# Gated cross-attention block: loads, first pass, heads' weights and last batch reordered, and normalised inputs turned in blocks through memory

## The chip, the cores and the metric

The kernel runs on one core of one Trainium2 chip. The metric is the device time of one execution in microseconds, the median of three runs. One core has five instruction streams that are spoken of here: TensorE (PE, matrix products; PEld is its weight load), VectorE (DVE), ScalarE (ACT), GpSimd (POOL) and SyncE (SP), which here only issues DMA transfers.

## The reference

The inputs are `x` of 32 batches x 256 tokens x 256 channels and `ctx_1024` of 32 x 77 x 256, all float32. Cut to what matters (LN is a layer norm without gain, `proj(t) = (LN(t) * ln_g + ln_b) @ w_in.T` split into 8 heads of 128):

```python
f_q, f_k = proj(LN(x)), proj(ctx)          # values are the keys' features
cosine = f_q . f_k / (|f_q| |f_k|)
ratio  = 2*min(var,1)/(var+1)              # per token and head, of queries and of keys
var_component = outer(q_ratio, k_ratio)
decorr = exp(-5 * norm(offdiag(cov of f_q over ALL tokens)) / 128**2)    # per head
cw, vw, ww = softmax(mlp(mean of f_q, mean of f_k over ALL tokens))      # per head
mixed  = cw*cosine + vw*cosine*decorr + ww*var_component
x = x + tanh(g_xattn) * ((mixed @ f_k) @ w_out.T + b_out)

q, k, v = LN(x)@Wq, LN(x)@Wk, LN(x)@Wv     # 16 heads of 16
z = softmax(k.q / 16) @ v @ Wo             # softmax over queries, per key
z = gelu(l2norm(l2norm(z) @ Wff))
x = x + tanh(g_ffn) * z
```

The weights of the three components depend on sums over all tokens of all batches. So a first pass over the whole of `x` and `ctx` has to be finished before any batch can be.

## The kernel before

**Order of work.** All compute instructions are issued through a helper (class `InOrder`, line 30, which is why the profile gives line 30 for nearly all) that keeps the order of the program on each engine. Only DMA issues on SP may be placed by the scheduler. So the order in which stages are called is the order in which each engine meets them. A stage is a function of a batch `b`; `run(b, stage, ...)` calls it once.

**Buffers.** PSUM has three tiles called `mm` (512 columns each) that all products take in turn: the fourth use waits until the first is read out. Two more tile pairs, `sc`, hold attention scores, one, `zp`, the mixed values.

**First pass** (lines 678 to 961). `x` is loaded two batches at a time (`load_group`, eight buffers). For each of 64 row blocks of 128 tokens (two to a batch) DVE takes statistics (`x_stats`), POOL turns them into scales for four blocks (`x_scales`), ACT normalises (`x_norm`), PE adds the block to the 256 x 256 Gram matrix `gram` (`x_gram`). Other first-pass work is put between by a table, `between`: transposes of `w_in` and `w_out`, statistics, norm and transposes of the context in five pieces (`ctx_stats`, `ctx_norm`, `ctx_transpose` into `kT_all`), loads of the last layers' weights, centring of `w_in` (`centre_w_in`). Small parameters are loaded at the start by SP, after `w_out` and two pieces of context.

**Heads' weights** (lines 966 to 1136). From the Gram matrix come the covariance (`correlate`, `square_up`), the softmax of the three weights and the factor `aw`. Stages of batches 0 and 1 are called between these, and then a list of stages brings batch 0 up to its second attention.

**Main loop** (lines 1176 to 1243). The list `cycle` is run through once for each batch in its second attention; entries name how far ahead another batch is. A turn has, in order, scores and exponents of the present batch in four quarters (`scores`, `exponents`, `scale_values`, `mix_values`), the last layers of the previous one (`ff_out`, `ff_norm_first`, `ff_norm_second`, `ff_gelu`, `ff_add`), the first attention of the next (`query_ratios`, `query_scores`, `attend`, `ff_stats`, `ff_norm`, `ff_transpose`, `ff_project`, `ff_values`) and features of the one after (`transpose_inputs`, `query_features`, `scale_queries`, `turn_queries`, `weigh_keys`, `scale_keys`, `transpose_keys`, `key_outputs`); `key_features`, `norm_inputs`, `measure_keys` and `align_keys` are for three ahead.

**The stages the change touches.** `norm_inputs` (195): POOL normalises the batch into `xn`. `transpose_inputs` (206): four PE transposes of 128 x 128 into an `mm` tile, two DVE passes that apply gain and bias into `xTc`. `query_features` (372): products of `xTc` with `winT` into `fq`, read out by ACT (first half) and DVE (second). `key_features` (225): the same for keys into `fvx`, by ACT. `measure_keys` (243): statistics of keys, eight `bn_stats` and small DVE work, and one power on POOL into `nrx`; it has work only when a block of 128 key rows is full. `align_keys` (253): DMAs that bring a batch's 77 keys to partition 0 (`fv`, `nr`). `turn_queries` (404): for batches from 2 on, DVE transposes blocks of 32 x 32 (`fb`), one DMA writes them to memory (`fd`), four read them back into place (`fqT`). `ff_norm_first` (601): a power on POOL gives `i1`, two ACT squares of `u` use it. `query_scores` (353): its read-outs into `s` are by ACT, DVE, ACT. `ff_gelu` and `warm_exponentials` (617, 623): the GELU and a dry exponential, each of which brings a table load on ACT.

Of the kernel before, what the change touches and what calls it, by code (L numbers as in the profile page):

```python
# [33 lines left out]
def gated_block_kernel(  # L34
# [171 lines left out]
    def transpose_inputs(b):  # L206
        k = kept[b]
        pt = transpose_in(k["xn"])
        xT = pa.tile([P, 2, S], F32, tag="xTc", name="xTc", bufs=1)
        for c in range(2):  # L210
            dve.tensor_scalar(
                xT[:, c, :], pt[:, c * S : (c + 1) * S], gcol[:, c : c + 1],
                bcol[:, c : c + 1], ALU.mult, ALU.add,
            )
        k["xTc"] = xT
# [347 lines left out]
    def mix_values(b, u):  # L563
        k = kept[b]
        g, kt = u // 2, u % 2
        if u == 0:
            k["zp"] = ps_z.tile([P, 2, S], F32, tag="zp", name="zp")
        es = [k.pop(("e", u, jp)) for jp in range(2)]
        for i in range(2):
            for j in range(4):  # L570
                pe.matmul(
                    k["zp"][32 * j : 32 * j + 32, g, :],
                    lhsT=vzs[u % 2][:, j, 2 * i : 2 * i + 2, :].rearrange("p i d -> p (i d)"),
                    rhs=es[j // 2][:, j % 2, i, :],
                    start=(i == 0 and kt == 0),
                    stop=(i == 1 and kt == NT - 1),
                )
        if u == 3:
            zT = pa.tile([P, 2, S], F32, tag="zT", name="zT", bufs=1)
            dve.tensor_copy(zT, k.pop("zp"))  # L580
            k["zT"] = zT
# [51 lines left out]


# [44 lines left out]
    load_group(1)  # L679
    load_group(2)  # L680
    load_w_in(0)
    load_group(3)
    load_w_in(1)
    load_ctx(0)
    load_w_out()
    load_ctx(1)

    grow = sw.tile([P, D], F32, name="grow")
    nc.sync.dma_start(out=grow, in_=ln_g.partition_broadcast(P))
    w1_n = sw.tile([P, D], F32, name="w1_n")  # L690
    nc.sync.dma_start(out=w1_n, in_=wp_w1)
    w2_n = sw.tile([3, P], F32, name="w2_n")
    nc.sync.dma_start(out=w2_n, in_=wp_w2)
    b1_r = sw.tile([1, P], F32, name="b1_r")
    nc.sync.dma_start(out=b1_r, in_=wp_b1.unsqueeze(0))
    b2_r = sw.tile([1, 3], F32, name="b2_r")
    nc.sync.dma_start(out=b2_r, in_=wp_b2.unsqueeze(0))
    bo_n = sw.tile([1, D], F32, name="bo_n")
    nc.sync.dma_start(out=bo_n, in_=b_out.unsqueeze(0))
    wpg = sw.tile([H, P], F32, name="wpg")  # L700
    nc.sync.dma_start(out=wpg, in_=wp_ln_g.partition_broadcast(H))
    wpb = sw.tile([H, P], F32, name="wpb")
    nc.sync.dma_start(out=wpb, in_=wp_ln_b.partition_broadcast(H))
# [11 lines left out]
    def x_stats(g):  # L715
        for k in range(4 * g, 4 * g + 4):
# [4 lines left out]
    def x_scales(g):  # L721


        cols = slice(4 * g, 4 * g + 4)
# [31 lines left out]
    def ctx_stats(g):  # L756
# [12 lines left out]
        mvs[g] = mv, r  # L769

    def ctx_norm(g):
        ct = cts[g]
        mv, r = mvs[g]
        for t, rows in ctx_parts(g):
            (dve if t < 2 else pool).tensor_scalar(
                ct[0:rows, t, :], ct[0:rows, t, :], mv[0:rows, t, 0:1], r[0:rows, t : t + 1],
                ALU.subtract, ALU.mult,
            )
# [74 lines left out]
    def centre_w_in(c):  # L853
        if c == 0:
            wcs.append(sw.tile([P, 2, HD], F32, tag="wB", name="wc"))
# [5 lines left out]
            wcs[0][:, c, :].rearrange("p (h d) -> p h d", d=P),  # L861
# [28 lines left out]
    def set_constants():  # L890
# [21 lines left out]
        for vz in vzs:  # L912
# [5 lines left out]
        1: [(transpose_w_in, 0, 0), (transpose_w_in, 1, 0), (load_ff, (w_of[:, :, 0:D], Wo))],  # L918
        2: [(ctx_stats, 0), (transpose_w_in, 0, 1), (transpose_w_in, 1, 1)],
        3: [(ctx_norm, 0), (transpose_w_out, 0), (transpose_w_out, 1)],  # L920
        4: [(ctx_stats, 1), (transpose_w_out, 2), (transpose_w_out, 3)],
        5: [(ctx_norm, 1), (ctx_transpose, 0, 0), (ctx_transpose, 0, 1), (load_ctx, 2)],
        6: [(centre_w_in, 0), (load_ff, (wf_n, Wff))],
        7: [(ctx_transpose, 1, 0), (ctx_transpose, 1, 1), (load_ctx, 3), (ctx_stats, 2)],
        8: [(ctx_norm, 2), (transpose_wo,)],
        9: [(ctx_stats, 3), (transpose_predictor,)],
        10: [(ctx_norm, 3), (ctx_transpose, 2, 0), (ctx_transpose, 2, 1), (load_ctx, 4)],
        11: [(centre_w_in, 1), (multiply_wo_wff,)],
        12: [
            (ctx_transpose, 3, 0), (ctx_transpose, 3, 1), (ctx_stats, 4),  # L930
            (load_ff, *((ffw[n], w) for n, w in zip("qkv", (Wq, Wk, Wv)))),
        ],
        13: [(ctx_norm, 4), (gate,)],
        14: [(ctx_transpose, 4, 0), (ctx_transpose, 4, 1), (lay_out_bias,)],
    }

    for g in range(-2, NG):
        if g + 2 < NG:
            x_stats(g + 2)
            x_scales(g + 2)  # L940
        if g == -1:
            for k in range(3):
                x_norm(k)
        if g < 0:
            continue
        extra = between.get(g, [])
        for i in range(4):
# [4 lines left out]
            if i < len(extra):  # L952
                stage, *which = extra[i]
                stage(*which)
        if g + 4 < NG:
            load_group(g + 4)
        elif g + 4 < NG + 2:
            for b in (2 * (g + 4 - NG), 2 * (g + 4 - NG) + 1):
                run(b, load_queries)
        if g == NG - 2:  # L960
            run(0, norm_inputs)

    wc = wcs[0]
# [13 lines left out]
    dve.tensor_copy(bl[:, :, 1], lb[:, :, 0])  # L977
    pt = mm_tile()
# [3 lines left out]
    lbT = sw.tile([P, 2 * D], F32, tag="fc", name="lbT", bufs=2)[0:2]  # L982
# [8 lines left out]
    run(0, transpose_inputs)  # L991
    run(1, norm_inputs)
    pt = mm_tile()
# [14 lines left out]
    run(0, query_features, 0, 0)  # L1008
    pt = mm_tile()
# [17 lines left out]
    y = sw.tile([P, 2, HD], F32, tag="wA", name="y")  # L1027

    def correlate(co, hh):
        cs = slice(hh * 512, (hh + 1) * 512)  # L1030
        pt = mm_tile()
        for c in range(2):
            pe.matmul(
                pt, lhsT=gs[:, c, co * P : (co + 1) * P], rhs=wc[:, c, cs],
                start=(c == 0), stop=(c == 1),
            )
        if co == 0:
            dve.tensor_copy(y[:, co, cs], pt)
        else:
            act.copy(y[:, co, cs], pt)  # L1040
# [30 lines left out]
    def square_up(hh):  # L1071
        pt = mm_tile()
        for i in range(4):
            hs = slice((hh * 4 + i) * P, (hh * 4 + i + 1) * P)
            for c in range(2):
                pe.matmul(
                    pt[:, i * P : (i + 1) * P], lhsT=wc[:, c, hs], rhs=y[:, c, hs],
                    start=(c == 0), stop=(c == 1),
                )
        fc = sw.tile([P, 4, P], F32, tag="fc", name="fc", bufs=2)  # L1080
# [29 lines left out]
    run(0, query_features, 1, 1)  # L1110
    pt = mm_tile()
# [6 lines left out]
    run(0, key_features)  # L1118
    run(0, measure_keys)
    run(0, align_keys)  # L1120

# [3 lines left out]
    pool.tensor_tensor(hw, hw, phalf, ALU.pow)  # L1125
    dg = sw.tile([H, 2, H], F32, name="dg")
# [3 lines left out]
    run(0, turn_queries, 0)  # L1130
# [9 lines left out]
    run(0, scale_queries, 1)  # L1140
    run(1, query_features, 0, 0)
    run(0, transpose_keys, 0)
    run(0, transpose_keys, 1)
    run(1, query_features, 0, 1)
    for pair in (2, 0, 1):
        run(0, key_outputs, pair)
    run(1, key_features)
    run(0, turn_queries, 1)
    run(0, query_ratios)
    for pair in range(3):  # L1150
# [5 lines left out]
    run(0, ff_norm, 0)  # L1156
    run(1, query_features, 1, 0)
    run(0, attend, 1)
    run(0, ff_stats, 1)
    run(0, ff_norm, 1)  # L1160
    run(1, query_features, 1, 1)
    run(1, weigh_keys)
    run(1, scale_keys)
    run(1, scale_queries, 0)
    run(1, scale_queries, 1)
    run(0, ff_transpose)
    run(0, ff_project, "k")
    run(0, ff_project, "q")
    run(0, ff_values)

# [9 lines left out]
        (2, transpose_inputs),  # L1180
# [3 lines left out]
        (0, exponents, 0, 1),  # L1184
        (2, query_features, 0, 0),
# [13 lines left out]
        (2, scale_queries, 0),  # L1199
        (2, query_features, 1, 0),  # L1200
# [5 lines left out]
        (2, turn_queries, 0),  # L1206
# [5 lines left out]
        (-1, ff_gelu),  # L1212
        (2, warm_exponentials),
# [8 lines left out]
        (1, ff_transpose),  # L1222
        (0, scores, 3),
# [4 lines left out]
        (3, norm_inputs),  # L1228
        (2, turn_queries, 1),
        (3, measure_keys),  # L1230
        (3, align_keys),
# [5 lines left out]
        (0, scale_values, 3),  # L1237
        (-1, ff_add),
    ]
    for n in range(-4, B + 1):  # L1240
        for ahead, stage, *which in cycle:
# [36 lines left out]
```

## Time and profile before

| | |
|---|---|
| median of 3 runs | 1453.61 us (1453.37 to 1454.99) |
| the profiled execution, its own time | 1451.74 us |
| its span | 1450.0 us |
| busy PE, DVE, ACT, POOL | 1387.5, 1056.7, 906.3, 534.5 us |
| mean granted PE clock | 0.98 |
| bytes moved by DMA | 106.23 MB, 73 GB/s |
| first product of the Gram matrix, last | 9.1 us, 83.0 us |
| length of a turn of the main loop | 40.0 us (40.8 with a second half of keys) |
| first scores of the last batch, its last exponent, end | 1406.0, 1431.3, 1450.0 us |

The profile is of one execution on the chip. A row of the timeline reads: start, length, engine, line, operation, what it writes <- what it reads, and in brackets the idle time before it and what ended that. A row of the waits reads: who waited <- for whom, us in total, times, longest. A piece of the chain reads: start, length, engine and what it wrote. "xN" counts instructions; each float32 product is two of them. A matmul's length includes its way through the pipeline, so the starts, not the lengths, tell how PE's time is used.

### The profile page before, as it was taken

The page shows a single profiled execution, that of the slowest core. Times are in us where ns is not written, and L with a number is a line of the kernel's source. Part 1 is how long each engine was busy: PE and PEld are TensorE (multiplying, and loading weights), DVE is VectorE, ACT ScalarE, POOL GpSimd, SP SyncE. Part 2 cuts the span into 40 slices and gives each one's busy share as a digit, 9 for nine tenths or more (in the row PEclk, how much of TensorE's full clock was granted, in tenths as well). Part 3 has the DMA queues.
Part 4 walks back from the last instruction along what each step waited for, and adds up shares of the span by engine and source line. Part 5 has one row for each costly group of instructions (what it writes and reads, how often), then busy time and mean ns, then how long its engine had stood idle before and what let it go on. Part 6 is the DMA issues. An engine that isn't in the chain of part 4 may idle for free.

```text
span 1450.0 us, 25957 instructions
## 1 busy us (share of the span) xinstructions
PE 1387.5 (96%) x8833; PEld 812.5 (56%) x8833; DVE 1056.7 (73%) x3053; ACT 906.3 (63%) x2978; POOL 534.5 (37%) x660
## 2 busy tenths in 40 slices
PE   6898899999999999999999999999999999999985
PEld 5764555555555555555555555555555555555541
DVE  5734678787778787887777777778777777877743
ACT  4712356676666676667667667666666765766675
POOL 5922343343233333343333343433433333334210
PEclk9989999999999999999999999999999999999996
DMA  8500022211222222212222222222222211222100
GB/s 267 181 15 28 4 74 75 78 65 62 78 74 63 80 86 76 82 67 76 67 76 74 73 69 79 85 76 74 68 75 73 78 61 64 76 72 70 66 8 15
DMA packets 69395, 106.23 MB, mean 73 GB/s; under 512 B 10810, under 2 KB 46575, under 8 KB 69262
## 3 DMA queue, kind: packets, MB, share of 16 engines
q1 hardware_dynamic: 68430, 104.56, 22.2%
q8 instruction: 70, 1.15, 0.3%
q14 instruction: 63, 0.52, 0.1%
q10 hardware_dynamic: 832, 0.00, 0.0%
HBM read 54.44 MB, written 39.85 MB: 65 GB/s over the span
## 4 chain that ended last, share of the span: by engine, by line
PE 72%; ACT 14%; DVE 5%; issue 2%; DMA 1%; POOL 1%; SPq 0%; ACTq 0%; POOLq 0%
PE mm L30 56%; PE sc L30 10%; ACT e L30 7%; PE zp L30 7%; ACT L30 4%; DVE nm L30 3%; ACT u L30 1%; ACT fvx L30 1%; DMA fd<-fb 1%; POOL rs L30 0%; ACT dry L30 0%; DVE fb L30 0%; DVE qst L30 0%; DMA fqT<-fd 0%; ACT ge L30 0%
## 5 line engine op out<-in xcount | busy, mean ns | idle before, releaser
L30 ACT ACTIVATE e<-sc,nm 128x256 f32<-128x256 f32 x1024 | 472.7, 485 | 200.3 <-DVE nm L30 200.3
L30 DVE TENSOR_REDUCE nm<-sc 128x4 f32<-128x1024 f32 x256 | 301.4, 1219 | 50.6 <-PE sc L30 50.6
L30 PE MATMUL mm<-winT,xTc 128*128 128x512 f32 x512 | 237.5, 606 | 2.6 <-DVE xTc L30 2.6
L30 ACT ACTIVATION_READ_ACCUMULATOR e<-sc,nm 128x1 f32 x1024 | 221.6, 216 | 0.0
L30 POOL TENSOR_TENSOR rq<-qt,nhalf 128x8 f32<-128x8 f32 x64 | 105.3, 1645 | 272.2 <-DVE qt L30 272.2
L30 PEld LDWEIGHTS mm<-winT,xTc 128*128 128x128 f32 x512 | 95.1, 191 | 120.9 <-issue 93.2
L30 PE MATMUL sc<-q,kTf 32*128 32x512 f32 x1024 | 154.3, 648 | 5.8 <-ACT e L30 5.8
L30 PE MATMUL mm<-vw,s 128*128 128x256 f32 x640 | 146.8, 384 | 0.0
L30 PE MATMUL zp<-e,vz 128*32 128x256 f32 x2048 | 139.7, 391 | 5.1 <-DVE vz L30 4.4
L30 POOL TENSOR_SCALAR i<-nn 128x2 f32<-128x2 f32 x64 | 14.1, 221 | 344.4 <-ACT ge L30 344.4
L30 PEld LDWEIGHTS mm<-vw,s 128*128 128x128 f32 x640 | 119.0, 190 | 28.5 <-issue 13.7
L30 POOL TENSOR_TENSOR fq<-fq,rq 128x1024 f32<-128x1024 f32 x64 | 121.4, 1897 | 5.0
L30 PE MATMUL mm<-w_of,zT 128*128 128x512 f32 x256 | 117.9, 604 | 0.8 <-DVE zT L30 0.8
L30 PEld LDWEIGHTS zp<-e,vz 128*32 128x32 f32 x2048 | 59.0, 111 | 95.5 <-issue 37.3
L30 DVE BATCH_NORM_STATS2 qst<-fq 128x6 f32<-128x128 f32 x512 | 104.7, 278 | 0.0
L30 PE MATMUL mm<-woutT,fvT 128*64 128x256 f32 (+2 forms) x1024 | 99.2, 383 | 0.6 <-DVE fvT L30 0.5
L30 PE MATMUL mm<-fqT,fvT 128*64 128x256 f32 (+2 forms) x1024 | 93.9, 383 | 1.0 <-DMA fqT<-fd 1.0
L30 POOL TENSOR_SCALAR rs<-mv 128x1 f32<-128x1 f32 x64 | 33.1, 517 | 166.8 <-DVE mv L30 132.7
L30 DVE RECIPROCAL sums<-sums 128x8 f32<-128x8 f32 x128 | 24.6, 192 | 92.4 <-ACT e L30 92.3
L30 ACT COPY vw<-mm 128x512 f32<-128x512 f32 x32 | 18.8, 586 | 115.7 <-PE mm L30 115.7
L30 ACT ACT_TABLE_LOAD x64 | 82.1, 1283 | 7.7 <-DMA x<-in_x_dram 4.3
L30 POOL TENSOR_SCALAR xn<-x,mv_x,rstd_x 128x256 f32<-128x256 f32 x64 | 78.9, 1239 | 10.3 <-issue 10.3
(204 smaller groups left out, 2286.2 us busy)
## 6 DMA issues: line engine op xcount, KB each, us to landing
fd<-fb SPq DMA_DIRECT2D x60, 512.0 KB
fqT<-fd SPq DMA_DIRECT2D x240, 128.0 KB
x<-in_x_dram SPq DMA_DIRECT2D x64, 256.0 KB
out_dram<-x SPq DMA_DIRECT2D x32, 256.0 KB
fv<-fvx SPq DMA_DIRECT2D x13, 308.0 KB
ct<-in_ctx_dram SPq DMA_DIRECT2D x4, 512.0 KB
w_in_n<-in_L_xattn_w_in_dram SPq DMA_DIRECT2D x2, 512.0 KB
w_out_n<-in_L_xattn_w_out_dram SPq DMA_DIRECT2D x1, 1024.0 KB
```

The costliest lines, as they stand in the source:

```text
L30: return lambda *args, **kw: self._tc.keep_in_program_order(method(*args, **kw))
```

## The change

- **First pass.** Loads: halves of `w_in` come earlier; `w_out`, the second context piece and the small parameters are called from the table `between` and no longer at the start; each group of `x` is called for after the second row block of a turn instead of after the fourth. Statistics and scales of the first four row blocks are made two by two. `ctx_norm` gives its four blocks to POOL, ACT, DVE, ACT (before: two to DVE, two to POOL), for which POOL works out a negative mean. The table has the context earlier: the last piece's norm stands in turn 12 and its transposes in turn 14 (before 13 and 14).
- **Heads' weights.** `wc`, `y`, `lbT` and `fc` move to other buffers, so that `fvx` is free sooner; key features, statistics and alignment of batch 0, its query turn and its keys' transposes are called earlier, as are stages of batches 1 and 2.
- **Inputs.** For batches from 3 on, `transpose_inputs` is a DVE block transpose of `xn` into `xb`, one DMA to memory (`xd`) and four DMAs back into `xq`. A new stage `gain_inputs` applies gain and bias on POOL, at the end of the turn. `norm_inputs` and `transpose_inputs` are called for three ahead.
- **Main loop.** `measure_keys` and `align_keys` are called near the start of a turn for two ahead (before: near its end for three ahead). `ff_gelu` and `warm_exponentials` stand behind `ff_transpose`. `turn_queries` stands behind `key_outputs` and behind the last `scale_values`.
- **Last batch.** It has a list of its own, `last`: scores ahead of mixing, the GELU of batch 30 after its last exponents. `zT` is copied in two halves, and a new stage `ff_finish` ends the batch one row block at a time.

```diff
     def transpose_inputs(b):
-        k = kept[b]
-        pt = transpose_in(k["xn"])
+        k = kept[b]
+        if b < 3:
+            k["xq"] = transpose_in(k["xn"]).rearrange("p (c s) -> p c s", c=2)
+            gain_inputs(b)
+            return
+        k["xq"] = pa.tile([P, 4, NT, 2, 32], F32, tag="xq", name="xq", bufs=1)
+        xb = pa.tile([P, 4, NT * 2, 32], F32, tag="xb", name="xb", bufs=1)
+        dve.transpose(
+            xb.rearrange("p j n a -> p n j a"),
+            k["xn"].rearrange("p t (c j a) -> p (t c) j a", c=2, a=32),
+        )
+        xd = dram.tile([P, 4, NT * 2 * 32], F32, tag="xd", name="xd")
+        nc.sync.dma_start(out=xd, in_=xb.rearrange("p j n a -> p j (n a)"))
+        for j in range(4):
+            nc.sync.dma_start(
+                out=k["xq"][32 * j : 32 * j + 32].rearrange("p i t c a -> p i (t c a)"),
+                in_=xd[:, j].rearrange("(i p) n -> p i n", p=32),
+            )
+
+    def gain_inputs(b):
...
         for c in range(2):
-            dve.tensor_scalar(
-                xT[:, c, :], pt[:, c * S : (c + 1) * S], gcol[:, c : c + 1],
-                bcol[:, c : c + 1], ALU.mult, ALU.add,
-            )
+            if b < 3:
+                engine, out, src = dve, xT[:, c, :], xq[:, c, :]
+            else:
+                engine = pool
+                out = xT[:, c, :].rearrange("p (t i a) -> p i t a", t=NT, a=32)
+                src = xq[:, :, :, c, :]
+            engine.tensor_scalar(
+                out, src, gcol[:, c : c + 1], bcol[:, c : c + 1], ALU.mult, ALU.add
+            )
...
     load_group(1)
+    load_w_in(0)
     load_group(2)
-    load_w_in(0)
+    load_w_in(1)
     load_group(3)
-    load_w_in(1)
     load_ctx(0)
-    load_w_out()
-    load_ctx(1)
...
-            (dve if t < 2 else pool).tensor_scalar(
...
+            if t % 2:
+                act.activation(c, c, AF.Identity, bias=nm[0:rows, t : t + 1], scale=r_t)
+            else:
+                (dve if t == 2 else pool).tensor_scalar(
...
     cycle = [
...
         (0, scores, 0),
-        (2, transpose_inputs),
+        (3, norm_inputs),
...
         (0, exponents, 0, 1),
+        (2, measure_keys),
+        (2, align_keys),
         (2, query_features, 0, 0),
...
         (2, scale_queries, 0),
+        (3, transpose_inputs),
         (2, query_features, 1, 0),
...
-        (2, turn_queries, 0),
         (1, attend, 0),
...
-        (-1, ff_gelu),
-        (2, warm_exponentials),
         (1, ff_norm, 0),
...
         (1, ff_transpose),
+        (-1, ff_gelu),
+        (2, warm_exponentials),
         (0, scores, 3),
...
         (2, key_outputs, 1),
-        (3, norm_inputs),
-        (2, turn_queries, 1),
-        (3, measure_keys),
-        (3, align_keys),
+        (2, turn_queries, 0),
         (0, exponents, 3, 0),
...
         (0, scale_values, 3),
+        (2, turn_queries, 1),
+        (3, gain_inputs),
         (-1, ff_add),
     ]
+
+    last = [
...
+        (0, exponents, 3, 1),
+        (0, scale_values, 3),
+        (0, mix_values, 3),
+        (-1, ff_gelu),
+        (0, ff_out, 0),
+        (0, ff_out, 1),
+        (-1, ff_add),
+        (0, ff_finish),
+    ]
-    for n in range(-4, B + 1):
-        for ahead, stage, *which in cycle:
+    for n in range(-4, B):
+        for ahead, stage, *which in last if n == B - 1 else cycle:
```

## The prediction

> **What bounds the kernel now.** I read the page first (shares, slices), then the list of waits, then one full turn of the main loop in the timeline, engine by engine, then the chain of work at both ends.
>
> ```profile
> PE 1387.5 (96%) x8833; PEld 812.5 (56%) x8833; DVE 1056.7 (73%) x3053; ACT 906.3 (63%) x2978; POOL 534.5 (37%) x660
> PE   6898899999999999999999999999999999999985
> PEclk9989999999999999999999999999999999999996
> ```
>
> The slices show three stages: of slices 1 to 5 (36 us each) only one is full, the next 33 are full of TensorE (PE) at full clock, the last two thin out. In the middle only PE time and PE stalls count. At the ends the order of work counts. The timeline of one middle turn, which starts at 768.74 us and lasts 40.0 us:
>
> ```profile
> 768.74 1.14 PE L30 MATMUL sc<-q,kTf 32*128 32x512 f32 x8
> 769.82 0.65 PE L30 MATMUL mm<-ident,xn 128*128 128x128 f32 x4
> 770.31 3.60 PE L30 MATMUL mm<-w_of,zT 128*128 128x512 f32 x8
> ...
> 778.78 2.93 PE L30 MATMUL mm<-fqT,fvT 128*64 128x256 f32 x32
> 781.53 1.05 PE L30 MATMUL zp<-e,vz 128*32 128x256 f32 x16
> 782.51 3.70 PE L30 MATMUL mm<-winT,xTc 128*128 128x512 f32 x8
> ```
> ```profile
> 774.82 0.72 POOL L30 TENSOR_TENSOR i<-i,nhalf 128x2 f32<-128x2 f32 x1
> ```
> ```profile
> 776.58 0.55 ACT L30 ACTIVATE ge<-u,i 128x256 f32<-128x256 f32 x1
> 779.92 0.59 ACT L30 COPY s<-mm 128x512 f32<-128x512 f32 x1 [2.21 <-PE mm L30]
> 782.21 0.39 ACT L30 COPY s<-mm 128x256 f32<-128x256 f32 x1
> ```
>
> Two things are to be seen. The four transposes of xn take 0.49 us of PE's issue (769.82 to 770.31), not the 0.65 printed, because matmuls overlap. And PE's query features at 782.51 reuse the PSUM tile that ScalarE (ACT) empties with the copy at 782.21: ACT's run from its copy at 779.92 to there (copy, four exponents, copy: 2.6 us) ends just when PE arrives. ACT has 2.21 us of idle time ahead of it, and no more.
>
> The ends, from the waits of the first 85 us and the last part of the chain:
>
> ```profile
> PE sc L30 <- ACT xna L30: 13.7, 5, 9.1
> DVE st L30 <- DMA x<-in_x_dram: 12.6, 4, 8.4
> ```
> ```profile
> 1424.06 1.28 ACT L30
> ...
> 1426.28 1.28 ACT L30
> 1427.56 0.01 issue
> 1427.58 3.77 ACT e L30 x16
> ...
> 1434.80 6.17 PE mm L30 x8
> ```
>
> VectorE (DVE) stood 8.4 us (14.8 to 23.2) for a load of x issued only at 20.6, behind eight small loads. In the tail two table loads for the GELU of batch 30 lie on the chain, between exponents of batch 31.
>
> **The change part by part.** Sums are made against the profiled execution (span 1450.0 us, its time 1451.7). The shown median of 1453.6 is 1.9 above that and keeps the distance.
>
> *Transposes off PE.* Batches 3 to 31: 29 x 0.49 = 14.2 us saved, if nothing else ends last. On DVE two evictions (0.99 us together) go and one block transpose comes. The row for twice the size (fb<-fq, 128x1024) has 1,235 ns, so 0.62 here; DVE had 1.0 us free just behind its new place. SP gets five more issues in a turn (about 0.4 each in the fqT rows), 2.1 us on a queue with some 6 us of issues in 40. The round trip, from the queries' own: 2.6 us from writing fd to the first read, 1.7 to issue four reads, 2.8 to land, 7.1 in all. The block is written near 17 us into a turn and scaled near 33, so 9 us are left over: nothing on the path.
>
> The Trainium skill ("VectorE: DVE Perf Modes", Rules for kernel authors) speaks against this: a 128x128 transpose belongs on TensorE when PSUM will do, and its section on the three transpose paths gives it 390 ns (bf16). Four at that price would be 1.56 us, or 45 us over 29 batches. The trace's 0.12 us of spacing is what PE gives back; I take 14.2.
>
> *Scale on GpSimd (POOL).* Two passes a batch; nearest row is xn<-x, 128x256, 1,239 ns, and at worst the 1,897 ns of fq<-fq: 2.5 to 3.8 us, behind the fq scaling and ahead of the next norm. POOL idles 10.0 us (764.5 to 774.5) just there. The Trainium skill ("GPSIMD Engine Reference", Engine selection) puts elementwise work on VectorE; DVE took 534 ns for this. On the path the difference would be 2 x 0.705 x 29 = 41 us slower. It is hidden: the result is due 5 us into the next turn and ready 2 before it. If that cover went, the 41 would come. I take 0.
>
> *Key statistics moved (measure_keys).* They stood where DVE idled (2.5 us at 764 to 767) and now come after DVE's two u copies, at 5.7 us into a turn. Of the 29 turns of the loop whose queue holds a previous batch's norm, 18 have such statistics. The query statistics are the same shape: 2.6 us of DVE from first to POOL's start. POOL's power nrx then takes 1.66 (its row: 31.6 us in 19). So it runs from 8.3 to 10.0. In POOL's order the power of i1 is queued behind it: its end moves from 6.8 to 11.0. In ACT's order the two squares of u wait for i1, and behind them stand the s copy, the exponents and the copy that frees PE's tile. Squares 11.0 to 12.0, copy to 12.5, exponents to 14.3, copy to 14.6. PE, 0.49 earlier, is there at 13.3. A stall of 1.3 us x 18 = 23.4 us lost. Bounds: 0.8 (ACT packs tighter) to 1.8 (further lateness in the next scores), 14 to 32. Other DVE work is late by 0.9 us at most there and recovers before the next maxima.
>
> *GELU moved behind the transpose of xf.* ACT's table loads and GELU (3.6 us) delayed its copy of fvx, for which PE waited 7.8 us in 21 turns. That stall goes, but PE then arrives earlier at the weights' fvT copy of DVE, which had 0.15 us to spare: I keep 5 of 7.8 (bounds 3 and 8). The cover for the moved 3.6 us is the ACT idle 3.4 us ahead of vw; without it the exponents of the last quarter would be late.
>
> *Second half of the query turn.* It is issued 4 us later, from -1.6 into the turn; by the 7.1 us above and its own 1.2 on DVE it lands at 6.8. PE wants it at 9.5. Slack 2.7, cost 0; before it was some 8. SP's output store stands between, with nothing to wait for but DVE.
>
> *First pass.* Small loads and w_out come later, x earlier. The x of group 4 then lands near 17 instead of 23, and the 3.6 us PE hole at 24 to 28 goes; PE should reach that group at 21, not 28: 7 us. From there DVE was 85 to 90% busy until 68 and set the pace. It loses 1.8 us of context norms, POOL loses 6 (5 x 1.24) and gains 5 x 0.4, ACT gains ten of its 0.6 us passes, for which its 25 to 30% of idle time there is the cover (6 us without it). Then PE waited for the last context block and ran at half clock: pieces from 68.2 to 83.0, where 7 rows of x at 0.7 us and two rounds of transposes need 6 at full clock. With the block's norm two groups ahead of its transposes I count 7 of those 9 us. Sum 14; bounds 7 (only the load) and 19.
>
> *Heads' weights and first batches.* Of the 85 us to 172, PE stood 12 us, the longest for dg (2.6), keys (1.7) and xTc (2.4). These three get other work between: 6.7. New waits behind DVE, now with statistics in that stretch, take some back; 5, bounds -1 to 9.
>
> *Last batch.* From its first scores to its last exponent: 25.4 us now (1406.0 to 1431.3). Re-stepped with 1.84 to 1.93 us for each of eight exponent groups, 1.9 for four squares and some 2 of first maximum and start, without GELU and its loads in between: 19.2, so 6 saved. The halved zT copy and the split final step save 1 more; PE's last products stay at 6.2 at half clock. 7, bounds 3 and 9.
>
> Sum: -14.2 + 23.4 - 5 - 14 - 5 - 7 = -21.8. So 1450.0 - 21.8 = 1428.2 for the span, and 1453.6 - 21.8 = 1431.8 for the median.
>
> **Rivals.** *(a) The statistics cost nothing:* ACT's 2.21 us of idle time absorb them, if POOL's power starts early. The order on POOL speaks against it. Then -45: 1408.
>
> *(b) The gain at the ends doesn't come:* the first pass stays with DVE, since its 50 us of work up to 72 us need every slot, and the prologue's holes only move. For it: DVE near 90% from 30 to 70 us. Then -14.2 + 23.4 - 5 - 7 (load only) - 4 = -7: 1447.
>
> *(c) Slower: the late half of the query turn.* If its landing takes more than 2.7 us over what I count, PE waits in each of some 28 turns. One write in the trace took 10.2 us instead of 2.6 (1206 us; another 8.6), and PE waited for it in spite of 8 us of slack. New traffic shares that queue. It turns the sign at 0.8 us a turn (21.8 / 28), that is, a landing 3.5 us late in each turn; at 3.7 us late the cost is 28 and the time 1460. Against it: of 60 writes, the 31 that had no other issue of SP behind them took 2.6 to 3.7 to the first read.
>
> *(d) The transposes don't give back their time,* because the same turn is held by ACT or DVE: for it, ACT meets PE at the query features. Then 14 less: 1446.
>
> **How the numbers follow.** Forecast 0.52 (own range 1420 to 1442), (a) 0.18, (b) 0.12, (d) 0.09, (c) 0.09. The range 1405 to 1449 leaves out (c), the far side of (a) and the tails of (b) and (d). A change within 0.2% (2.9 us) is about what a measurement of this kernel can't tell from none. Slower is (c) with a little of (b), less that part of (c) that ends near zero: 0.08; same 0.03; faster 0.89.
>
> **What the profile after would show.** No transposes of xn on PE from batch 3. In turns with nrx, ACT's squares wait for POOL near 3 us and PE stalls at its second query features by 1.3; in turns without, the period is 0.9 us or so shorter. No wait of PE for fvx. The first pass ends near 69 us; no 8 us hole of DVE. The last exponent comes 19 us after the last batch's first scores. Wrong if turns with statistics are as short as the others, if PE waits for fqT, or if the gain of the first pass is eaten before the main loop begins.

## The result and the profile after

The changed kernel takes **1428.9 us** (median of 4 runs, 1427.1 to 1431.2), the kernel before beside it 1453.5 (1452.4 to 1455.0). The ratio is 0.9831, 95% interval 0.9813 to 0.9849: 24.6 us less by the medians, 22 to 27 by the interval. The forecast was 1431.8. The profiled execution of the changed kernel took 1431.2 us, with a span of 1429.4 us; that of before had 1450.0. The spans, from which the forecast's terms were reckoned, differ by 20.6 us. The sum forecast was 21.8. One execution of e1 (1738.0 us) and one of e2 (2173.0 us) ran slow and are left out of their ratios; the only profile of e1 is of that execution, so e1 is read by its time alone.

The sum was nearly right, but three of its eight terms were not, as the views below begin to show. First the page of the changed kernel: busy times, and TensorE (PE) with its granted clock in 40 slices.

```profile
PE 1379.9 (97%) x8717; PEld 798.0 (56%) x8717; DVE 1047.9 (73%) x3021; ACT 911.5 (64%) x2986; POOL 564.2 (39%) x732
PE   7998999999999999999999899999999998999986
PEclk9999999999999999999999999999999999999996
```

PE executes 116 matmuls fewer: the transposes of 29 batches. The thin slices at the start have filled up in part. But in the 23rd and the 34th slice PE is not full, in the middle of the main loop, where before it was.

The lengths of the turns of the main loop, from the first product with `w_of` in each to the next, say where the time went:

| | before | after |
|---|---|---|
| end of the first pass (last Gram product) | 83.0 us | 70.5 us |
| from there to the first product with `w_of` | 126.4 us | 123.4 us |
| a turn (with a second half of keys) | 39.87 to 39.99 (40.92) us, the 29th 39.38 | 39.42 to 39.48 (40.42) us |
| single longer turns | 41.04 us | 45.47, 45.82, 40.67 us (the 16th, the 26th, the 20th) |
| turn of batch 30, turn of batch 31, and what follows | 34.4 + 27.8 + 15.2 us | 36.6 + 25.3 + 12.1 us |

Turns with key statistics and turns without are equally long. So the stall that the forecast gave to 18 turns is absent. Here is the place in the timeline of one of these 18 turns, which started at 834.0 us.

```profile
841.20 1.66 POOL L30 TENSOR_TENSOR nrx<-kt,nquart 128x8 f32<-128x8 f32 x1 [11.34 <-DVE kt L30]
...
844.01 0.51 ACT L30 ACTIVATE ge<-u,i 128x256 f32<-128x256 f32 x1 [3.49 <-POOL i L30]
...
845.00 0.56 ACT L30 COPY s<-mm 128x512 f32<-128x512 f32 x1
...
846.32 3.70 PE L30 MATMUL mm<-winT,xTc 128*128 128x512 f32 x8
...
847.28 0.38 ACT L30 COPY s<-mm 128x256 f32<-128x256 f32 x1
```

ScalarE (ACT) does wait 3.5 us for GpSimd (POOL), as forecast. But PE starts its second query features at 846.32, while the copy that was said to free their tile runs only from 847.28. So they must have taken another tile. ACT's first copy ended at 845.56, 0.76 us ahead of PE.

The waits of PE in the changed kernel:

```profile
PE mm L30 <- DMA fqT<-fd: 6.3, 2, 5.0
PE mm L30 <- DMA nr<-nrx: 4.3, 1, 4.3
...
PE mm L30 <- DVE fvT L30: 1.3, 6, 0.5
...
PE mm L30 <- ACT fvx L30: 1.1, 1, 1.1
```

The wait for `fvx` (7.8 us in 21 before) is gone but for one of 1.1 us. A wait for the query turn has come, in few places but long. The 4.3 us that the view puts down to `nr` belong to it too: the products that end this wait, in the row at 801.53 below, read `fqT`. SyncE's DMA issues show it at 773 to 797 us, ahead of and in the first of the two long turns:

```profile
773.08 3.52 SPq L291 DMA_DIRECT2D fv<-fvx  x2
783.08 0.35 SPq L457 DMA_DIRECT2D fd<-fb  x1
791.44 1.73 SPq L459 DMA_DIRECT2D fqT<-fd  x4
793.27 0.38 SPq L457 DMA_DIRECT2D fd<-fb  x1
...
796.84 1.75 SPq L459 DMA_DIRECT2D fqT<-fd  x4
```
```profile
801.53 4.54 PE L30 MATMUL mm<-fqT,fvT 128*64 128x256 f32 x32 [4.34 <-DMA nr<-nrx]
```

The write of the first query half was issued at 783.08, and the reads that wait for it came 8.4 us later. The second half, now called late, queued behind that: its write was issued at 793.27 and its reads at 796.84. The same is found at 1185.75 (8.7 us). The windows of this turn show the busy time of PE, PEld, DVE, ACT and POOL, then PE's granted clock, the DMA share and GB/s:

```profile
796.00:801.50 5.50, 1.19 (x10) 0.31 (x8) 3.52 (x6) 1.09 (x4) 3.67 (x7) 0.99 0.52 148
801.50:805.00 3.50, 3.47 (x16) 1.90 (x16) 0.00 (x0) 1.46 (x6) 0.00 (x0) 0.52 0.26 76
805.00:809.00 4.00, 4.00 (x39) 1.97 (x38) 3.73 (x20) 3.27 (x15) 0.66 (x1) 1.00 0.00 0
```

PE stands 4.3 us. Then its clock is 0.52 for 3.5 us, which costs 1.7 more. Together they make this turn 6.0 us too long.

### The profile page after: what moved, and what is told of

Read it like the earlier page. It is cut to its first block, busy times and chain, and to the rows that moved or that the text cites. A ratio compares the mean times of both kernels' runs of the same rounds, so it can differ in the third digit from the quotient of the medians.

```text
span 1429.4 us, 25911 instructions
## 1 busy us (share of the span) xinstructions
PE 1379.9 (97%) x8717; PEld 798.0 (56%) x8717; DVE 1047.9 (73%) x3021; ACT 911.5 (64%) x2986; POOL 564.2 (39%) x732
## 4 chain that ended last, share of the span: by engine, by line
PE 75%; DVE 12%; POOL 5%; DMA 4%; issue 2%; ACT 2%; SPq 1%; POOLq 0%; ACTq 0%
PE mm L30 59%; PE sc L30 9%; PE zp L30 7%; POOL rs L30 4%; DVE qst L30 3%; DVE qt L30 2%; DMA fd<-fb 2%; DVE st L30 2%; DVE xf L30 1%; ACT e L30 1%; DMA x<-in_x_dram 1%; DVE x L30 1%; DVE fvT L30 1%; DVE mv L30 1%; SPq L459 0%
## 5 line engine op out<-in xcount | busy, mean ns | idle before, releaser
L30 POOL TENSOR_TENSOR nrx<-kt,nquart 128x8 f32<-128x8 f32 (+1 forms) x20 | 33.2, 1659 | 224.8 <-DVE kt L30 224.8
L30 PE MATMUL mm<-woutT,fvT 128*64 128x256 f32 (+2 forms) x1024 | 111.2, 392 | 4.5 <-DVE fvT L30 1.3
L30 PE MATMUL mm<-fqT,fvT 128*64 128x256 f32 (+2 forms) x1024 | 98.5, 395 | 10.6 <-DMA fqT<-fd 6.3
L30 POOL TENSOR_SCALAR i<-nn 128x2 f32<-128x2 f32 (+1 forms) x66 | 14.6, 221 | 194.3 <-ACT ge L30 192.6
L30 PEld LDWEIGHTS mm<-fqT,fvT 128*64 128x64 f32 (+2 forms) x1024 | 48.7, 122 | 68.7 <-issue 46.8
L30 PEld LDWEIGHTS mm<-w_of,zT 128*128 128x128 f32 x256 | 46.5, 191 | 71.1 <-issue 46.7
```

The source lines that it names most:

```text
L30: return lambda *args, **kw: self._tc.keep_in_program_order(method(*args, **kw))
```

## Experiments

All medians are beside runs of the kernel before on the same chip. Differences in the text are differences of ratios times 1453.5 us, with the two intervals combined.

| run | what differs | median us | ratio to before, interval |
|---|---|---|---|
| changed kernel | | 1428.9 | 0.9831 (0.9813 to 0.9849) |
| e2 | changed kernel, `nrx` power twice | 1449.4 | 0.9978 (0.9969 to 0.9988) |
| e3 | changed kernel, transposes on PE | 1439.0 | 0.9914 (0.9892 to 0.9936) |
| e10 | changed kernel, gain on VectorE | 1443.2 | 0.9940 (0.9920 to 0.9959) |
| e9 | changed kernel, key transfers cut in two | 1416.5 | 0.9754 (0.9726 to 0.9782) |
| e4 | changed kernel, query turn early | 1412.6 | 0.9733 (0.9712 to 0.9754) |
| e1 | e4, key statistics at the old place | 1415.9 | 0.9749 (0.9727 to 0.9771) |
| e7 | e4, GELU at the old place | 1413.3 | 0.9745 (0.9710 to 0.9780) |
| e6 | e4, last batch by the ordinary list | 1420.3 | 0.9780 (0.9753 to 0.9807) |
| e5 | e4, loads of the start as before | 1419.4 | 0.9766 (0.9748 to 0.9785) |
| e8 | e4, context norm as before | 1418.8 | 0.9762 (0.9747 to 0.9776) |
| e12 | e4, `transpose_keys` ahead of the statistics | 1427.6 | 0.9825 (0.9805 to 0.9845) |
| e13 | e12 and the cut of e9 | 1425.9 | 0.9810 (0.9795 to 0.9825) |

### The query turn

```diff
         (0, mix_values, 1),
+        (2, turn_queries, 0),
         (1, attend, 0),
...
         (2, key_outputs, 1),
-        (2, turn_queries, 0),
+        (2, turn_queries, 1),
...
         (0, scale_values, 3),
-        (2, turn_queries, 1),
```

> The changed kernel with both turn_queries back at their old places (the first ahead of the first attention of the next batch, the second behind the keys' outputs). If the two turns of 45.5 us come from a write to memory of 8 us that the later place can't absorb: no turn over 42 us, 12 us faster than the profiled execution of the changed kernel and 6 to 12 faster than its median of 1428.9, so 1417 to 1423. If the late turns are an accident of single executions that hits any order: the same time. If VectorE's transposes at the old places delay the first attention: each turn up to 0.5 us longer, 1440.

The ratio falls by 0.0098: 14 us (10 to 18) off the changed kernel, somewhat more than was expected. In its profile the turns have 39.45 to 39.47 us, or 40.42 with a second half of keys, and none is out of line but the 29th (39.93); the turn of batch 30 has 34.0 us in place of 36.6. So the later call of `turn_queries`, which the forecast put at nothing, cost 14 us in the changed kernel. The two writes themselves are as late in e4 as before (8.4 and 9.0 us from the write to the first read), but the earlier call covers them. Why only a few turns, and always the same ones? In e2, e3 and e10 the long turns were the 16th and the 26th too, though e3 has five DMAs fewer per turn. What these share is a pair of key transfers of 73 and 55 rows, or of 71 and 57 (292 and 220 KB, 284 and 228 KB at 4 KB a row).

```diff
-            nc.sync.dma_start(out=k["fv"][at : at + n], in_=fvx[i % 4][row : row + n])
+            even = n // 16 * 16
+            for lo, hi in ((0, even), (even, n)):
+                if hi > lo:
+                    nc.sync.dma_start(
+                        out=k["fv"][at + lo : at + hi], in_=fvx[i % 4][row + lo : row + hi]
+                    )
```

> The changed kernel with each transfer of key features (align_keys, fv) cut in two: the largest multiple of 16 rows, then the rest; nothing else. If the two turns of 45.5 us come from the pieces of 73 and 71 rows (prime numbers), which one DMA engine carries alone at 26 GB/s for 11 us while the query turn's write waits behind them on that engine: no such turn, 12 us off the profiled execution and 11 to 14 off the median of 1428.9, so 1415 to 1418, and writes of fd of 2.6 to 3.7 us throughout. If the late writes have another cause: the same two turns, 1429. The one more issue of SyncE per batch (0.4 us) costs nothing by either.

11 us (6 to 16) off the changed kernel, and the two long turns are 39.44 us. The DMA view of 773 to 792 us (40 slices of 0.475 us, bytes moved per time) of the changed kernel:

```profile
GB/s 0 0 0 198 164 112 0 0 9 17 26 43 17 26 26 26 26 34 26 26 26 26 26 362 354 250 86 78 43 26 26 34 26 26 26 26 26 17 0 0
```

The same view of e9:

```profile
GB/s 0 0 0 17 95 233 104 43 0 0 121 190 259 112 0 0 0 0 0 0 0 0 0 0 52 423 414 216 0 0 13 175 289 267 263 267 321 427 380 311
```

In the first, one transfer trickles at 26 GB/s from 778 to 791 us. That is a sixteenth of the 423 that the write reaches in e9, and the DMA share there is 0.05 to 0.06: one engine of 16. The query write (362, 354, 250) comes while it runs. Most of the write is over in 1.5 us, but its last part lands only when the trickle ends. With the cut there is no trickle, and the reads follow after 2.6 us. So the long pieces as they stand are carried at the rate of one engine and hold back a later write. Does the row count decide it? The trace of the changed kernel has other counts, from the same stage. Here is a transfer of 24 rows (338 to 346 us, 40 slices of 0.2 us):

```profile
GB/s 0 0 0 0 0 0 0 0 164 102 205 21 0 0 0 0 0 0 0 0 0 0 0 0 0 0 0 0 0 0 0 0 0 0 0 0 0 0 0 0
```

And here is one of 23 rows (536.2 to 544.2 us):

```profile
GB/s 0 0 0 0 0 0 0 20 20 0 20 0 20 20 20 20 0 0 0 20 41 20 0 123 20 20 41 20 20 20 41 20 0 0 0 0 0 0 0 0
```

24 rows are through in 0.8 us, 23 rows take 5 (the slice of 123 holds another transfer too). The transfers of 47 and of 53 rows trickle in the same way, and the writes behind them took 3.6 and 3.5 us instead of 2.6, which the slack covered. All these counts (23, 47, 53, 71, 73) are prime, so no number of engines from 2 to 16 divides them. That the rows are dealt out to the engines in equal shares is the reading that fits these counts and the cut of e9; no view shows it directly.

### The key statistics

```diff
-        (2, measure_keys),
-        (2, align_keys),
...
+        (2, turn_queries, 0),
         (1, attend, 0),
...
         (2, key_outputs, 1),
-        (2, turn_queries, 0),
+        (2, turn_queries, 1),
+        (3, measure_keys),
+        (3, align_keys),
...
         (0, scale_values, 3),
-        (2, turn_queries, 1),
```

> The changed kernel with measure_keys and align_keys back behind the keys' outputs, three ahead, and both turn_queries back at their old places; to be read against the run with turn_queries alone put back (e4). Forecast's term (the statistics hold ScalarE 3.3 us and TensorE then stalls 1.3 us in 18 turns): 23 us faster than e4, about 1400. Rival (TensorE needs only the first of ScalarE's two score copies, which still comes 0.8 us ahead of it): no difference from e4 beyond 3 us.

Against e4 the ratio is 0.0016 higher: 2 us slower (between 2 faster and 7 slower). The 23 us are excluded. The second run, the changed kernel with one more power on POOL, asks how near the new place is to costing something.

```diff
-            pool.tensor_tensor(nr[:, 0:H], n2, nquart[0:rows], ALU.pow)
+            for _ in range(2):
+                pool.tensor_tensor(nr[:, 0:H], n2, nquart[0:rows], ALU.pow)
```

> The changed kernel with GpSimd's power for the key norms computed twice into the same place (+1.66 us on GpSimd ahead of the power of i1, in 18 turns of the loop that carry it). If the first score copy is what TensorE's second query features wait for, with 0.76 us of slack: a stall of 0.9 us in each of 18 turns, 16 us slower than the changed kernel, about 1445, and the turns with statistics 0.9 longer than the others. If the second copy counted (the forecast's reading): the whole 1.66 us in each, 30 us slower, about 1459. If ScalarE's lateness is absorbed altogether: no change, 1429.

21 us slower than the changed kernel (18 to 24). 15 turns are longer by 1.30 to 1.34 us, the two long ones and two more by 0.3 to 1.7, and those without statistics have 39.44 or 40.42 as in the changed kernel. The timeline of such a turn:

```profile
402.79 3.39 POOL L30 TENSOR_TENSOR nrx<-kt,nquart 128x8 f32<-128x8 f32 x2 [12.32 <-DVE kt L30]
...
408.32 0.56 ACT L30 COPY s<-mm 128x512 f32<-128x512 f32 x1
...
408.94 3.70 PE L30 MATMUL mm<-winT,xTc 128*128 128x512 f32 x8 [0.61 <-ACT s L30]
...
410.59 0.38 ACT L30 COPY s<-mm 128x256 f32<-128x256 f32 x1
```

PE now waits for ACT, starts 0.06 us after the first copy ends, and doesn't wait for the second. So the chain from POOL over ACT to PE is real, and it is the first copy that counts. The changed kernel has 0.76 us in hand there. In all, PE waits 14.8 us in 16 such places, 0.9 each. The turns grew by 0.4 us more than that. PE's starts, set side by side with those of the changed kernel, show where: the features begin 1.03 us later, and the mixed values behind the third scores 1.31 later. That second 0.28 us is a wait for DVE's `vz`, whose sums wait for ACT's late exponents.

### The transposes and the gain

```diff
-        if b < 3:
+        if True:
             k["xq"] = transpose_in(k["xn"]).rearrange("p (c s) -> p c s", c=2)
...
         (0, scores, 0),
+        (2, transpose_inputs),
         (3, norm_inputs),
...
-        (3, transpose_inputs),
...
-        (3, gain_inputs),
```

> The changed kernel with the inputs of all batches turned on TensorE into PSUM and scaled on VectorE at the old place, without the block transpose and the round trip through memory; all else as changed. If the turns give back the transposes' 0.49 us each and nothing else: 39.94 us a turn in place of 39.47, 13.6 us slower, about 1442. If the round trip of the inputs also delays the query turn's transfers on the same queue: the turns that are 6 us long go too, and it is at most 8 slower. If the turn was held by ScalarE or VectorE anyway: the same time.

12 us slower (8 to 16). The turns have 39.87 us, or 40.81 with a second half of keys, and the two long ones stay. So the transposes off PE are worth 0.40 to 0.42 us a turn. That is less than the 0.49 of the forecast; about 0.1 us of that is lost again just behind them: from the first product with `w_of` to the first query features it is 3.43 us in the kernel before (770.31 to 773.74) and 3.54 in the changed one (834.01 to 837.55). The round trip of the inputs has no part in the late writes.

```diff
-                engine = pool
+                engine = dve
```

> The changed kernel with the gain of the turned inputs on VectorE in place of GpSimd, at the same place in the program. VectorE's end of turn has no slack in the trace (reciprocal, values, block transpose, ff_add, zT from 831.03 to 833.95, and TensorE's w_of starts at 834.01): two passes of 0.53 us make every turn 1.06 us longer, 31 us slower, about 1459. If VectorE has room there after all: 1429. If other work of the turn absorbs half of it: 1444.

16 us slower (12 to 20): half of what the idle time of VectorE (DVE) suggested. The passes were shorter than expected, 0.39 us each from `xq` and not 0.53 as from PSUM before, and of these 0.78 us a turn 0.65 count: a turn has 40.10 us. The waits of PE in e10 name the victim:

```profile
PE mm L30 <- DVE zT L30: 16.3, 28, 0.6
```

On POOL the two passes took 1.09 us (0.55 each) and hold up nothing. The engine with the idle time was the right one for this step. The rule that the prediction weighed, elementwise work on VectorE (the Trainium skill, "GPSIMD Engine Reference", Engine selection), fits the single pass (0.39 against 0.55 us), but at this place it would have cost 16 us.

### The GELU

```diff
         (0, exponents, 2, 1),
+        (-1, ff_gelu),
+        (2, warm_exponentials),
         (1, ff_norm, 0),
...
         (1, ff_transpose),
-        (-1, ff_gelu),
-        (2, warm_exponentials),
```

> The kernel of e4 (1412.6 us) with ff_gelu and warm_exponentials back at their old place ahead of the last norm of the first attention. Forecast's term (the wait of TensorE for fvx, 7.8 us in 21 turns, comes back, and 5 of it counts): 1418. Rival (the turn with transposes on TensorE of e3 was 39.87 against 39.93 before, so the wait for fvx only took the place of another of the same length): within 2 us of e4, 1411 to 1415.

2 us slower than e4, within an interval of 6, and the turns have 39.46 us in both. The waits of PE's weight loads show how. First e7, with the GELU at the old place:

```profile
PEld mm L30 <- ACT fvx L30: 12.6, 24, 1.4
PEld mm L30 <- DVE fvT L30: 1.5, 2, 1.0
```

Then e4, with the GELU at the new place:

```profile
PEld mm L30 <- DVE fvT L30: 14.4, 24, 0.6
...
PEld mm L30 <- ACT fvx L30: 1.4, 1, 1.4
```

24 waits for ACT's `fvx` have turned into 24 waits for DVE's `fvT`, a few products further on. PE's starts say the same. Counted from the first product with `w_of` of the 11th turn, the products with `woutT` start at 28.97 us in e7 and at 28.39 in e4, and the group behind them at 32.00 in both. The move gave nothing. If that wait is the last obstacle, taking it away gives 13 to 16 us more:

```diff
-        (2, scale_queries, 1),
         (2, transpose_keys, 0),
         (2, transpose_keys, 1),
+        (2, scale_queries, 1),
```

> The kernel of e4 (1412.6 us) with transpose_keys called ahead of the second scale_queries, so that VectorE copies fvT before the query statistics and not after them. Theory: the move of the GELU took away TensorE's wait for ScalarE's fvx copy (0.35 us and what it drags along), and in the 22 turns with one half of keys TensorE then waits as long for this fvT copy of VectorE (0.62 us at its weight load in the trace of e4). Then these turns become 0.6 to 0.75 us shorter, 38.7 to 38.85 in place of 39.46, and the kernel 13 to 16 faster, 1397 to 1400. Rival (TensorE is full in every turn and 39.46 is its work): 1411 to 1415.

It came out 13 us slower than e4 (9 to 18). The wait for `fvT` is gone and a longer one stands in its place:

```profile
PEld mm L30 <- DVE vw L30: 42.4, 30, 1.4
```

DVE copies `fvT` at 618.97 in the turn at 612 us, but the statistics, which it used to do while PE was busy, now lie between that copy and the maxima. The sum into `vw` comes behind the maxima (624.67), and PE needs the tile that it empties. The turns have 39.73 us, and 41.45 with a second half of keys (40.42 before). So my theory that one wait stood alone fell: DVE has hardly any free time between the second norm and `vw`, and whichever of its results comes last there is what PE waits for.

> The kernel of e12 with the key transfers cut in two as in e9. With the early query turn the long single-engine transfers are covered, so the cut should give nothing more: as e12 within 2 us. If a late write still costs in some turns of e12: up to 3 us faster than it.

2 us faster than e12 (between 6 faster and 1 slower): nothing that can be told from none.

### Both ends

```diff
     load_group(1)
-    load_w_in(0)
     load_group(2)
-    load_w_in(1)
+    load_w_in(0)
     load_group(3)
+    load_w_in(1)
     load_ctx(0)
+    load_w_out()
+    load_ctx(1)
...
+    load_small()
...
-        2: [(transpose_w_in, 0, 1), (transpose_w_in, 1, 1), (load_w_out,), (load_small,)],
-        3: [(ctx_norm, 0), (load_ctx, 1)],
+        2: [(transpose_w_in, 0, 1), (transpose_w_in, 1, 1),],
+        3: [(ctx_norm, 0)],
```

> The kernel of e4 (1412.6 us) with the loads of the start in their old order: w_in later, w_out, the second context piece and the small parameters ahead of the fifth group of x; all other work of the first pass stays as changed. Forecast's term for the load alone: VectorE's 8 us wait for x comes back and the first pass ends 7 us later, 1420. Rival (the first pass is set by the rate of VectorE's or of the loads' total, not by this hole): within 2 us of e4.

5 us slower than e4 (1 to 9); the first pass ends at 75.0 us and not at 70.3. DVE's waits for x are 12.1 us in 5, the longest 5.0, against 8.3 in 7, the longest 2.6.

```diff
-            if t % 2:
-                act.activation(c, c, AF.Identity, bias=nm[0:rows, t : t + 1], scale=r_t)
-            else:
-                (dve if t == 2 else pool).tensor_scalar(
-                    c, c, mv[0:rows, t, 0:1], r_t, ALU.subtract, ALU.mult
-                )
+            (dve if t < 2 else pool).tensor_scalar(
+                c, c, mv[0:rows, t, 0:1], r_t, ALU.subtract, ALU.mult
+            )
...
-        12: [(ctx_norm, 4), (lay_out_bias,)],
+        12: [(lay_out_bias,)],
+        13: [(ctx_norm, 4)],
```

> The kernel of e4 (1412.6 us) with the context's norms split over VectorE and GpSimd again as before (two and two, none on ScalarE) and the last piece's norm one turn of the first pass later, one ahead of its transposes. Forecast's term for the last context block: TensorE's wait for GpSimd and half clock at the end of the first pass come back, 7 us slower, 1420. Rival (the norm now comes soon enough at the later place too): within 2 us, 1411 to 1415.

4 us slower (1 to 8) by the ratio, and in the profile the first pass ends 6.0 us later, at 76.3. The run puts both the split of the norms and their place back, so it doesn't tell which of the two did it. The rows of its end show the old waits for POOL again (e8, PE):

```profile
67.83 0.33 PE L30 MATMUL mm<-ident,ct 128*128 128x128 f32 x1 [0.75 <-POOL ct L30]
69.03 0.24 PE L30 MATMUL mm<-ident,ct 32*128 32x32 f32 x1 [0.87 <-POOL ct L30]
```

```diff
-        if b == B - 1 and u % 2:
-            if u == 1:
-                k["zT"] = pa.tile([P, 2, S], F32, tag="zT", name="zT", bufs=1)
-            dve.tensor_copy(k["zT"][:, g, :], k["zp"][:, g, :])
-        elif u == 3:
+        if u == 3:
...
-    for n in range(-4, B):
-        for ahead, stage, *which in last if n == B - 1 else cycle:
+    for n in range(-4, B + 1):
+        for ahead, stage, *which in cycle:
```

> The kernel of e4 (1412.6 us) with the last batch run through the ordinary list again (no list of its own, zT copied whole, last step not split). Forecast's term for the tail: 7 us slower, 1420. From the lengths of the last two turns and what follows (before 34.4 + 27.8 + 15.2 = 77.4; in e4's profile 34.0 + 25.4 + 11.9 = 71.3): 6 slower, 1419. If the list of its own gives nothing: 1413.

7 us slower than e4 (2 to 12): the forecast's 7.

## Why the prediction was right, and where it was not

The time, 1428.9 against 1431.8, is within the forecast's range. Its terms, for the spans of the two profiled executions:

| term | forecast us | measured us | from |
|---|---|---|---|
| transposes off PE | -14.2 | -13.2 | 28 turns x 0.47, of which 0.41 by e3; the rest not traced |
| gain on POOL | 0 | 0 | no wait for it; e10 |
| key statistics moved | +23.4 | 0 | e1, e2 |
| GELU moved | -5 | 0 | e7 |
| second half of the query turn | 0 | +15 | 12.4 in two turns, 2.6 in that of batch 30; e4, e9 |
| first pass | -14 | -12.5 | 83.0 to 70.5 |
| heads' weights | -5 | -3.0 | 126.4 to 123.4; no run for it alone |
| last batch | -7 | -5.6 | 44.1 to 38.5 from its first scores to the end; e6 |
| sum | -21.8 | -19.3 | spans: -20.6 |

What is left, 1.3 us, is mostly the one longer turn of before (41.04, 1.1 too long), where PE waited 1.0 us for `fqT`; its cause is the one in the row on the query turn.

*Right in mechanism and size.* The transposes gave back most of their spacing on PE, not the 45 us that the Trainium skill's 390 ns each would have made by the prediction's estimate ("VectorE: DVE Perf Modes", the three transpose paths), and the gain on POOL was hidden. The first pass gave nearly what was counted: the load of x and the context norm each did their part (4.7 and 6.0 us at the end of the first pass; 7 and 7 forecast).

*Key statistics: the step that failed is "PE's query features at 782.51 reuse the PSUM tile that ScalarE (ACT) empties with the copy at 782.21".* I took the three `mm` tiles to go round strictly, as the section on buffers has it, and the short distance between the two times for a dependence. The rows that the prediction shows speak against it: the copy starts at 782.21 and takes 0.39 us, so it ends at 782.60, 0.09 us after the features that were to wait for it. It is so in every turn of that trace but the first. The tile held for `query_scores` of the last pair is held longer, and the features take the one freed by ACT's first copy. The rest of the step happened as written. Counted as in the prediction from the turn's first scores, here at 832.93, POOL's power started at 8.3 us, ACT's squares at 11.1, and its two copies ended at 12.6 and 14.7 (forecast 8.3, 11.0, 12.5 and 14.6). The stall forecast for 18 turns became 0.76 us of slack in 18 turns, and e2 shows that 1.66 us more would have made it true. So rival (a) had this term right in its result, but not in its reason: POOL didn't start early and ACT was 3.5 us late, which PE didn't feel. Its time, 1408, did not come, because of the next one.

*Query turn: the step that failed is "it lands at 6.8. PE wants it at 9.5. Slack 2.7, cost 0".* It is right for all turns but three. The profile of before had two writes of 8.6 and 10.2 us, which I set aside as outliers in rival (c). They weren't accidents, as SyncE's issues in the kernel before show:

```profile
796.61 2.07 SPq L263 DMA_DIRECT2D fv<-fvx  x2
805.16 0.35 SPq L429 DMA_DIRECT2D fd<-fb  x1
...
813.72 1.73 SPq L431 DMA_DIRECT2D fqT<-fd  x4
...
1197.80 2.05 SPq L263 DMA_DIRECT2D fv<-fvx  x2
1206.35 0.34 SPq L429 DMA_DIRECT2D fd<-fb  x1
...
1216.63 2.71 SPq L431 DMA_DIRECT2D fqT<-fd  x4
```

They stand behind the same two pairs of key transfers (220 and 292 KB, 228 and 284 KB), which every execution has. I priced (c) as a delay in each turn, whereas it came as two delays of 6 us, and a smaller one in the turn of batch 30, where PE waited 1.4 us and then ran at a mean clock of 0.66 for 5 us. That one stays in e9 (36.6 us), so the cut does not touch it.

*GELU: "I keep 5 of 7.8" should have been 0.* The prediction names the replacement, DVE's `fvT` copy with 0.15 us to spare, but gives it only part of the gain.

*Heads' weights* is a term mis-sized by 2 us. *Last batch*: near in sum (5.6 of 7), but not in its parts. The exponents ended 23.7 us after the first scores, not 19.2, so 1.7 of the 6 came: with PE at half clock from 1398.8 to 1419.2 (`zp` in 1.94 us in place of 1.07), ACT waited 4.0 us in five places for its products and for the maxima behind them. What follows the last exponent fell from 18.7 to 14.8, by 3.9 and not 1. Of that 1.5 came from the clock: it was back at full from 1419.2, so the last products took 4.6 us and not the 6.2 of the forecast.

The errors in the key statistics (23 too pessimistic) and in the query turn and the GELU (20 too optimistic) cancelled. The number owes its precision to that, which is luck.

The kernel of e4, the change with both query turns left where they were, beats both: 1412.6 us, 0.9733 of the kernel before.

## What to carry to other kernels

A write or read that takes three times its usual time in a trace should be followed to what was issued ahead of it before it is called an accident: if its cause is in the program, it returns in every execution, and slack that covers it is not free to give away. When a change takes a wait away from a full engine, look for the next result that it needs within a microsecond, and count the gain only up to there. A dependence through a rotating buffer should be read from when the one ends and the other starts, in several places, not from two times that happen to lie close.

## What the runs showed of the hardware that was not expected

- Copies of 73 and 71 rows of 4 KB from one place in SBUF to another moved at 26 GB/s, a DMA share of one engine in 16; cut at a multiple of 16 rows, the same bytes were through 5.5 us after the issue. A later write that used all engines was held for 8.4 us in place of 2.6. 23 rows took 5 us where 24 took 0.8.
- A standstill of PE of 4.3 us was followed by 3.5 us at a granted clock of 0.52. Two of 0.9 and 1.4 us within 4 us (the turn of batch 30) were followed by 5 us at a mean of 0.66. So in these places the clock added about 1.7 us.
- POOL's `tensor_scalar` with two columns took 0.55 us for 128x256 in the gain (multiply, add, strided input) and 1.24 in `xn` (subtract, multiply).
